# Softmax reciprocals of the first layer taken back from HBM as a tenth row instead of being spread by matmuls

## The chip, the cores and the metric

The kernel runs on one core of a Trainium2 chip. Its time is the device time of one execution in microseconds (us); a figure for a kernel is the median of several executions. The engines are called TensorE (PE in the profile, PEld where it loads weights), VectorE (DVE), ScalarE (ACT), GpSimd (POOL) and SyncE (SP, which issues the DMAs). All arithmetic is in 32-bit floats.

## The reference, cut to what matters

The network has four layers on two images of 512 channels by 64 x 64 pixels. The change touches only the first, an attention in which every pixel looks at its 3 x 3 neighbours (nine "taps") and at 256 pooled tokens. Both share one softmax, and to the weights of the nine taps a learned term is added:

```
attn_local = einsum('bhnd,bhndk->bhnk', q_scaled, k_local)          # 9 per pixel and head
attn_pool  = einsum('bhnd,bhpd->bhnp', q_scaled, l2norm(k_pool))    # 256 per pixel and head
attn = softmax(concatenate([attn_local, attn_pool], axis=-1), axis=-1)
a_local, a_pool = attn[..., :9], attn[..., 9:]
lt = einsum('bhnd,hdk->bhnk', q_norm, learnable_tokens) + learnable_bias + a_local
x_local = einsum('bhnk,bhndk->bhnd', lt, v_local)
x_pool  = einsum('bhnp,bhpd->bhnd', a_pool, v_pool)
out = (x_local + x_pool) @ W_proj + b_proj
```

There are 8 heads of 64 channels, so 128 channels (one partition each) hold two heads.

## The kernel before

The first layer of an image is cut into 16 units: four blocks of 128 channels by four stretches of 1024 pixels. It runs in **turns**. In one turn several generators, each working on another unit, are advanced in rotation, one `yield` at a time; one such rotation is a **step**, and a turn has ten of them, numbered 0 to 9 here. While `attend` works on unit u, `weigh` finishes unit u-1 and the projections prepare u+3 and u+4.

```
for i in range(-4, units + 1):
    k, q, ahead, u, before = (unit(i + n) for n in (4, 3, 1, 0, -1))
    stages = [norms, tap_products(ahead), attend(u), weigh(before), tap_sums(ahead), projections, normed, ...]
    in_turn(*stages)          # in rotation, one yield of each at a time
...
class Local: ...
    self.taps = [two parts of a lent buffer, one of its own]      # ring of three, 128 x 1024 each
    self.recip = part.take([P, TB])                               # TB = 512
def bank(self):               # a PSUM bank out of a pool of five
    return self.pp.tile([P, TB], F32, name="mm")
```

`attend` makes the exponentials of the pooled scores, their product with the values (`out`, not divided yet), and at step 7 the sum of all exponentials for each pixel and head, with the sums on 128 rows of `psD`: row 64j + r holds the pixels of half j, of head r mod 2. The exponentials of the taps, `el`, lie in 4 blocks of 32 rows; in each block the rows from 18 on belong to no tap. Their exponents are 0 and their learned term `lt` is 0, so after the two VectorE operations below such a row holds just the reciprocal.

```
    psD = sums()                                    # step 7 of attend
    for i in range(2):
        part = slice(i * TB // 2, (i + 1) * TB // 2)
        nc.vector.reciprocal(self.recip[:, part], psD[:, part])
    yield
    el = self.el.pop(u)                             # step 8
    nc.vector.tensor_tensor(el, el, self.recip, ALU.mult)
    nc.vector.tensor_tensor(el, el, self.lt.pop(u), ALU.add)
    self.spread = self.rows()                       # 64 x 1024 in HBM
    for j in range(2):
        nc.sync.dma_start(self.spread[:, j * TB:(j + 1) * TB], el[j * HD:(j + 1) * HD, :])
    self.fetch_tap(0)
    yield
    self.fetch_tap(1)                               # step 9
    yield

def fetch_tap(self, k):       # one HBM row to the 64 channels of each head
    at = 32 * (k % 2) + 2 * k
    for h in range(2):
        self.nc.sync.dma_start(self.taps[k % 3][h * HD:(h + 1) * HD, :],
                               bcast(self.spread[at + h], 0, HD))
```

`weigh`, a turn later, divides the pooled part by the sums, with the reciprocals spread over the channels by two matmuls of 2 rows, and adds the nine taps. A tap's weights are first copied by ScalarE into PSUM, then VectorE multiplies them with the shifted values `vx`, and GpSimd adds the product to `out`.

```
def weigh(self, u):
    out, R = self.out.pop(u), self.recip
    self.fetch_tap(2)
    yield                                           # end of step 0
    banks = [self.bank() for _ in range(2)]
    for j, ps in enumerate(banks):
        q = slice(64 * j, 64 * j + 2)
        nc.tensor.matmul(ps, self.cst[q, C_ROW:C_ROW + P], R[q, :], start=True, stop=True)   # L2260
    for j, ps in enumerate(banks):
        o = out[:, j * TB:(j + 1) * TB]
        nc.vector.tensor_tensor(o, o, ps, ALU.mult)                                          # L2263
    for k in range(9):                              # step 1 + k
        banks = [self.bank() for _ in range(2)]
        for ps, part in zip(banks, parts):
            nc.scalar.copy(ps, part)                                                         # L2270
        for j, (ps, part) in enumerate(zip(banks, parts)):
            nc.vector.tensor_tensor(part, vx[shifted by dy, dx], ps, ALU.mult)               # L2273
        nc.gpsimd.tensor_tensor(out, out, self.taps[k % 3], ALU.add)                         # L2277
        if k + 3 < 9:
            self.fetch_tap(k + 3)
        if k < 8:
            yield
    nc.sync.dma_start(self.yd[:, cc, lo:lo + self.UT], out)                                  # L2283
```

Other lines that the profile names: L133 the projections (128 x 128 weights, 512 columns), L1976 the output projection in the last turns, L2048 and L2055 the norms, L2138 and L2151 the tap products and their sums, L2183 and L2187 the pooled scores and their exponentials, L2193 the pooled values, L2230 the reciprocals, L2237 the store of the rows, L2247 the fetch of a tap. A 32-bit matmul stands as two instructions in the profile, so the two matmuls of L2260 are four records.

Of the kernel before, what the change touches and what calls it, by code (L numbers as in the profile page):

```python
# [11 lines left out]
ALU = mybir.AluOpType  # L12
# [3 lines left out]
P = 128  # L16
# [4 lines left out]
TB = 512  # L21
# [3 lines left out]
HD = 64  # L25
# [16 lines left out]
def bcast(ap, axis, n):  # L42

    a = ap.unsqueeze(axis)
    shape = list(a.shape)
    shape[axis] = n
    return a.to_broadcast(shape)
# [10 lines left out]
class General:  # L58
# [130 lines left out]
    def layer0(self, X, Y, sp_scale, tokT, d):  # L189
        tc, nc, vec = self.tc, self.nc, self.vec  # L190
        with tc.tile_pool(name="l0", bufs=1) as sp:
# [7 lines left out]
            with tc.tile_pool(name="l0b", bufs=2) as wp, \  # L199
                    tc.tile_pool(name="l0s", bufs=2, space=PSUM) as pps, \  # L200
                    tc.tile_pool(name="l0m", bufs=3, space=PSUM) as pp, \
                    tc.tile_pool(name="l0o", bufs=1, space=PSUM) as ppo:
                taps = wp.tile([18, 9, P], F32, name="taps", bufs=1)
                nc.sync.dma_start(taps, d["taps"])
                steps = []
                for cc in range(KC):
                    steps += self.local_chunk(X, Y, cc, xs, nmean, rstd, sp_scale, tokT, taps, d,
                                              wp, pps, pp, ppo)
                in_turn(steps[0][0]())
                for i, (_, attend) in enumerate(steps):  # L210
                    ahead = [steps[i + 1][0]()] if i + 1 < len(steps) else []
                    in_turn(attend(), *ahead)
# [63 lines left out]
    def local_chunk(self, X, Y, cc, xs, nmean, rstd, sp_scale, tokT, taps, d, wp, pps, pp, ppo):  # L276
# [137 lines left out]
        def attend(blk):  # L414
# [48 lines left out]
            nc.vector.tensor_tensor(Y[:, cc, blk * TB:(blk + 1) * TB], acc, psO, ALU.add)  # L463

        return [(lambda b=b: prepare(b), lambda b=b: attend(b)) for b in range(NB)]


# [1232 lines left out]
class Local:  # L1700
# [469 lines left out]
    def attend(self, u):  # L2170

        nc = self.nc
        cc = u // self.UN
        qs, el = self.qs[u % 3], self.el[u]
        out = self.att()
        prob = {}
        self.out[u] = out
        heads = [slice(h * HD, (h + 1) * HD) for h in range(2)]

        def exponentials(j, k2):  # L2180
            pS = [self.bank() for _ in range(2)]
            for h, c in enumerate(heads):
                nc.tensor.matmul(pS[h], self.kp[c, cc, k2 * P:(k2 + 1) * P],  # L2183
                                 qs[c, j * TB:(j + 1) * TB], start=True, stop=True)
            prob[j, k2] = [self.prob() for _ in range(2)]
            for h in range(2):
                nc.scalar.activation(prob[j, k2][h], pS[h], AF.Exp)  # L2187

        def values(j):
            psO = self.bank()  # L2190
            for k2 in range(2):
                for h, c in enumerate(heads):
                    nc.tensor.matmul(psO[c, :], self.vp[:, k2, cc * P + h * HD:][:, :HD],  # L2193
                                     prob[j, k2][h], start=(k2 == 0), stop=(k2 == 1))
            nc.scalar.copy(out[:, j * TB:(j + 1) * TB], psO)
            dst = prob[1, 1] if j else self.halves
            for h in range(2):
                nc.gpsimd.tensor_tensor(dst[h], prob[j, 0][h], prob[j, 1][h], ALU.add)  # L2198

        def sums():  # L2200
            psD = self.bank()
            blocks = [slice(j * HD, (j + 1) * HD) for j in range(2)]
            for h in range(2):
                for j, b in enumerate(blocks):
                    nc.tensor.matmul(psD[b, :], self.cst[:, C_EVEN + h:C_EVEN + h + HD],
                                     (prob[1, 1] if j else self.halves)[h], start=(h == 0),
                                     stop=False)
            for b in blocks:
                nc.tensor.matmul(psD[b, :], self.cst[b, C_SD:C_SD + HD], el[b, :], start=False,
                                 stop=True)  # L2210
            return psD

        exponentials(0, 0)
        yield
        exponentials(0, 1)
        yield
        values(0)
        yield
        exponentials(1, 0)
        yield  # L2220
        exponentials(1, 1)
        yield
        values(1)
        yield
        yield
        psD = sums()
# [5 lines that stand above are left out]
        el = self.el.pop(u)  # L2232
        nc.vector.tensor_tensor(el, el, self.recip, ALU.mult)
        nc.vector.tensor_tensor(el, el, self.lt.pop(u), ALU.add)
        self.spread = self.rows()
        for j in range(2):
            nc.sync.dma_start(self.spread[:, j * TB:(j + 1) * TB], el[j * HD:(j + 1) * HD, :])  # L2237
        self.fetch_tap(0)
        yield
        self.fetch_tap(1)  # L2240
        yield

    def fetch_tap(self, k):

        at = 32 * (k % 2) + 2 * k
        for h in range(2):
            self.nc.sync.dma_start(self.taps[k % 3][h * HD:(h + 1) * HD, :],  # L2247
                                   bcast(self.spread[at + h], 0, HD))

    def weigh(self, u):  # L2250

        nc = self.nc
        cc, y0 = u // self.UN, u % self.UN * self.UY
        out, R = self.out.pop(u), self.recip
        self.fetch_tap(2)
        yield
        banks = [self.bank() for _ in range(2)]
        for j, ps in enumerate(banks):
            q = slice(64 * j, 64 * j + 2)
            nc.tensor.matmul(ps, self.cst[q, C_ROW:C_ROW + P], R[q, :], start=True, stop=True)  # L2260
        for j, ps in enumerate(banks):
            o = out[:, j * TB:(j + 1) * TB]
            nc.vector.tensor_tensor(o, o, ps, ALU.mult)  # L2263
        for k in range(9):
            dy, dx = divmod(k, 3)
            parts = [self.taps[k % 3][:, j * TB:(j + 1) * TB] for j in range(2)]

            banks = [self.bank() for _ in range(2)]
            for ps, part in zip(banks, parts):
                nc.scalar.copy(ps, part)  # L2270
            for j, (ps, part) in enumerate(zip(banks, parts)):
                y = y0 + dy + j * self.UY // 2
                nc.vector.tensor_tensor(  # L2273
                    part.rearrange("p (y x) -> p y x", x=W),
                    self.vx[:, y:y + self.UY // 2, dx:dx + W],
                    ps.rearrange("p (y x) -> p y x", x=W), ALU.mult)
            nc.gpsimd.tensor_tensor(out, out, self.taps[k % 3], ALU.add)  # L2277
            if k + 3 < 9:
                self.fetch_tap(k + 3)
            if k < 8:  # L2280
                yield
        lo = u % self.UN * self.UT
        nc.sync.dma_start(self.yd[:, cc, lo:lo + self.UT], out)  # L2283
        yield
# [160 lines left out]
```

## Time and profile before

| what | value |
|---|---|
| time, median of 3 runs | 5462.01 us (5449.31 to 5468.27) |
| span of the profiled execution | 5449.6 us |
| mean granted TensorE clock | 0.969 of full speed |
| busy: TensorE, VectorE, ScalarE, GpSimd | 5161.0, 3144.7, 1793.0, 1803.2 us |
| first layer's turns with `weigh` in them, image 0 | from about 350 to 1075 us of the span |
| the same, image 1 | from about 3054 to 3776 us |
| distance from one turn's L2260 to the next, most turns | 45.86 us |

Busy times are unions of the records of an engine. The profile shows matmuls pipelined, with modelled ends, so two of them overlap in the records; where TensorE is concerned, the start of one group to the start of the next tells more than the length of a record. An instruction's "idle before" is the time that its engine stood still ahead of it, with the instruction that ended the wait.

### The profile page before, as it was taken

The page shows a single profiled execution, that of the slowest core. Times are in us where ns is not written, and L with a number is a line of the kernel's source. Part 1 is how long each engine was busy: PE and PEld are TensorE (multiplying, and loading weights), DVE is VectorE, ACT ScalarE, POOL GpSimd, SP SyncE. Part 2 cuts the span into 40 slices and gives each one's busy share as a digit, 9 for nine tenths or more (in the row PEclk, how much of TensorE's full clock was granted, in tenths as well). Part 3 has the DMA queues.
Part 4 walks back from the last instruction along what each step waited for, and adds up shares of the span by engine and source line. Part 5 has one row for each costly group of instructions (what it writes and reads, how often), then busy time and mean ns, then how long its engine had stood idle before and what let it go on. Part 6 is the DMA issues. An engine that isn't in the chain of part 4 may idle for free. (4 is left out here: it accounts for less than half of the span.)

```text
span 5449.6 us, 51666 instructions
## 1 busy us (share of the span) xinstructions
PE 5161.0 (95%) x18891; PEld 2254.2 (41%) x18891; DVE 3144.7 (58%) x3918; ACT 1793.0 (33%) x3409; POOL 1803.2 (33%) x1198
## 2 busy tenths in 40 slices
PE   7999999999988899999999999998999889999998
PEld 4423332554333344544444333335543334445443
DVE  3256667745679633565532566676456895334565
ACT  1245555233212233212212455542432131332221
POOL 0025556401310045444400355554012101554443
PEclk9999999999989999999989999999999899999999
DMA  3024445500000000211110344455000000000111
GB/s 141 2 62 122 128 126 154 153 18 24 1 1 0 1 1 1 82 35 57 51 55 2 81 126 125 124 154 154 1 24 0 1 0 1 1 8 20 38 36 42
DMA packets 113563, 293.27 MB, mean 54 GB/s; under 512 B 17234, under 2 KB 30034, under 8 KB 111252
## 3 DMA queue, kind: packets, MB, share of 16 engines
q1 hardware_dynamic: 113300, 289.88, 18.1%
q8 instruction: 151, 2.47, 0.2%
q14 instruction: 112, 0.92, 0.1%
HBM read 241.32 MB, written 48.50 MB: 53 GB/s over the span
## 5 line engine op out<-in xcount | busy, mean ns | idle before, releaser
L133 PE MATMUL mm<-big,w 128*128 128x512 f32 x2560 | 1188.4, 609 | 5.2 <-DVE late L2230 5.1
L133 PEld LDWEIGHTS mm<-big,w 128*128 128x128 f32 x2560 | 467.8, 191 | 687.4 <-issue 590.3
L2277 POOL TENSOR_TENSOR late<-late,big 128x1024 f32<-128x1024 f32 x192 | 454.7, 2368 | 298.6 <-DVE big L2273 285.3
L1265 POOL TENSOR_TENSOR total<-prob 128x512 f32<-128x512 f32 x128 | 159.6, 1269 | 759.3 <-ACT prob L1262 759.3
L1182 PE MATMUL acc<-big,dg 128*128 128x512 f32 x704 | 320.0, 613 | 59.0 <-DVE big L697 25.9
L1624 POOL TENSOR_SCALAR qf_sum<-qf,ksum_ratio 128x512 f32<-128x512 f32 x128 | 198.8, 1562 | 511.1 <-ACT qf L1674 353.8
L1437 POOL TENSOR_TENSOR big<-big 128x512 f32<-128x512 f32 x224 | 277.8, 1271 | 235.0 <-ACT big L1428 235.0
L2198 POOL TENSOR_TENSOR late<-late 128x512 f32<-128x512 f32 x128 | 160.6, 1276 | 487.1 <-ACT late L2187 448.2
L697 DVE TENSOR_TENSOR big<-big 128x3968 f32<-128x3968 f32 x72 | 308.8, 4289 | 6.9 <-ACT big L698 0.9
L2273 DVE TENSOR_TENSOR big<-big,mm 128x512 f32<-128x512 f32 x384 | 254.7, 679 | 85.1 <-ACT mm L2270 84.3
L1428 ACT ACTIVATE big<-mm,ed 128x256 f32<-128x256 f32 x512 | 193.7, 488 | 276.5 <-DVE top L1424 248.8
L2270 ACT COPY mm<-big 128x512 f32<-128x512 f32 x384 | 220.6, 594 | 161.4 <-DMA big<-rows 123.7
L1362 PE MATMUL mm<-proj,k 64*128 64x256 f32 x2048 | 268.9, 393 | 0.9 <-ACT k L1329 0.9
L1282 DVE RECIPROCAL recip<-psD 128x512 f32<-128x512 f32 x64 | 214.9, 3357 | 87.2 <-PE psD L1279 87.2
L1655 PE MATMUL mm<-k,w 128*128 128x512 f32 x512 | 242.0, 612 | 14.1 <-DVE k L1648 14.1
L1583 DVE TENSOR_REDUCE tops<-mm 128x2 f32<-128x512 f32 x256 | 161.5, 684 | 160.2 <-PE mm L1362 159.9
L1262 ACT ACTIVATE prob<-mm 128x512 f32<-128x512 f32 x256 | 132.0, 605 | 364.4 <-PE mm L1259 359.2
L1362 PEld LDWEIGHTS mm<-proj,k 64*128 64x128 f32 x2048 | 206.5, 188 | 105.7 <-issue 90.1
L2138 DVE TENSOR_TENSOR prod<-qs,big 128x1024 f32<-128x1024 f32 x192 | 230.5, 1215 | 30.7 <-PE tap L2151 29.1
L2277 POOL TENSOR_TENSOR late<-late,tap 128x1024 f32<-128x1024 f32 x96 | 226.5, 2360 | 64.4 <-DVE tap L2273 45.7
L133 PE MATMUL mm<-big,big 128*128 128x512 f32 x512 | 238.9, 629 | 0.0
L2151 PE MATMUL tap<-prod,cst 128*32 128x512 f32 x768 | 226.7, 612 | 9.9 <-DVE prod L2138 9.8
(364 smaller groups left out, 8300.2 us busy)
## 6 DMA issues: line engine op xcount, KB each, us to landing
big<-rows SPq DMA_DIRECT2D x384, 256.0 KB
tap<-rows SPq DMA_DIRECT2D x192, 256.0 KB
yd<-late SPq DMA_DIRECT2D x32, 512.0 KB
lost_all<-lost SPq DMA_DIRECT2D x128, 128.0 KB
out<-big SPq DMA_DIRECT2D x64, 256.0 KB
big<-in_W_kv SPq DMA_DIRECT2D x8, 1024.0 KB
rows<-late SPq DMA_DIRECT2D x64, 128.0 KB
big<-yd SPq DMA_DIRECT2D x16, 512.0 KB
```

Of the source, the lines that this page charges most:

```text
L133: self.nc.tensor.matmul(ps, w[:, kc, :], X[:, kc, blk * TB:(blk + 1) * TB], start=(kc == 0), stop=(kc == KC - 1))
L697: nc.vector.tensor_tensor(o, a, b, ALU.max)
L1182: nc.tensor.matmul(accs[b], dg, src[:, b * TB:(b + 1) * TB], start=(j == 0), stop=(j == 6))
L1282: nc.vector.reciprocal(r, psD)
L1362: nc.tensor.matmul(pS[h][i][:, t, :], k[lo:lo + HD, tok:tok + P], proj[lo:lo + HD, :], start=True, stop=True)
L1437: nc.gpsimd.tensor_tensor(a, a, part, ALU.add)
L1655: nc.tensor.matmul(ps, self.wo[:, kc, oc * P:(oc + 1) * P], qs[:, kc, :], start=(kc == 0), stop=(kc == KC - 1))
L2138: self.nc.vector.tensor_tensor(self.prods[k % 3].rearrange("p (y x) -> p y x", x=W), qs, self.kx[:, y + dy:y + dy + self.UY, dx:dx + W], A ...
L2151: nc.tensor.matmul(ps[32 * q:32 * q + 32, :], self.cst[:, C_TAPW + 16 - 2 * k:C_TAPW + 48 - 2 * k], self.prods[k % 3][:, j * TB:(j + 1) * ...
L2270: nc.scalar.copy(ps, part)
L2273: nc.vector.tensor_tensor(part.rearrange("p (y x) -> p y x", x=W), self.vx[:, y:y + self.UY // 2, dx:dx + W], ps.rearrange("p (y x) -> p y ...
L2277: nc.gpsimd.tensor_tensor(out, out, self.taps[k % 3], ALU.add)
```

## The change

The reciprocals are no longer spread by matmuls. As rows 20 and 21 of the stored rows hold them already, they are fetched back from HBM onto the 128 channels like a tap, and a turn of `weigh` handles ten rows in ten steps instead of nine in nine: the reciprocals in step 0, tap k in step k + 1 as before. The ring of three buffers stays, and turns on by one place from unit to unit, since ten is no multiple of three. The aim is to take the two matmuls off TensorE and to start `weigh` in the turn's first step.

```
-        self.fetch_tap(0)
-        yield
-        self.fetch_tap(1)
-        yield
+        self.fetch_tap(u, 0)
+        yield
+        self.fetch_tap(u, 1)
+        yield

-    def fetch_tap(self, k):
-        at = 32 * (k % 2) + 2 * k
+    def fetch_tap(self, u, i):
+        at = 32 * ((i - 1) % 2) + 2 * (i - 1) if i else 20
+        t = self.taps[(10 * u + i) % 3]
         for h in range(2):
-            self.nc.sync.dma_start(self.taps[k % 3][h * HD:(h + 1) * HD, :],
-                                   bcast(self.spread[at + h], 0, HD))
+            self.nc.sync.dma_start(t[h * HD:(h + 1) * HD, :], bcast(self.spread[at + h], 0, HD))

     def weigh(self, u):
-        out, R = self.out.pop(u), self.recip
-        self.fetch_tap(2)
-        yield
-        banks = [self.bank() for _ in range(2)]
-        for j, ps in enumerate(banks):
-            q = slice(64 * j, 64 * j + 2)
-            nc.tensor.matmul(ps, self.cst[q, C_ROW:C_ROW + P], R[q, :], start=True, stop=True)
-        for j, ps in enumerate(banks):
-            o = out[:, j * TB:(j + 1) * TB]
-            nc.vector.tensor_tensor(o, o, ps, ALU.mult)
-        for k in range(9):
-            dy, dx = divmod(k, 3)
-            parts = [self.taps[k % 3][:, j * TB:(j + 1) * TB] for j in range(2)]
+        out = self.out.pop(u)
+        self.fetch_tap(u, 2)
+        for i in range(10):
+            t = self.taps[(10 * u + i) % 3]
+            parts = [t[:, j * TB:(j + 1) * TB] for j in range(2)]
             banks = [self.bank() for _ in range(2)]
             for ps, part in zip(banks, parts):
                 nc.scalar.copy(ps, part)
+            dy, dx = divmod(i - 1, 3)
             for j, (ps, part) in enumerate(zip(banks, parts)):
+                if i == 0:
+                    o = out[:, j * TB:(j + 1) * TB]
+                    nc.vector.tensor_tensor(o, o, ps, ALU.mult)
+                    continue
                 ... (the tap's multiplication, as before)
-            nc.gpsimd.tensor_tensor(out, out, self.taps[k % 3], ALU.add)
-            if k + 3 < 9:
-                self.fetch_tap(k + 3)
-            if k < 8:
+            if i:
+                nc.gpsimd.tensor_tensor(out, out, t, ALU.add)
+            if i + 3 < 10:
+                self.fetch_tap(u, i + 3)
+            if i < 9:
                 yield
```

## The prediction

> **What bounds the kernel now.** I read the page first, then the busy times by stretch, then the kernel's lines that the change touches, and last the order of time over one turn. The page gives 95% to TensorE over the whole span, which hides the stages, so the stretch of nine even turns of image 0 comes next. Columns: stretch, its length, busy us and records of PE, PEld, DVE, ACT, POOL, clock, DMA share, GB/s.
>
> ```profile
> 440.00:854.00 414.00, 412.93 (x1482) 133.15 (x1480) 284.43 (x450) 232.96 (x406) 235.95 (x118) 1.00 0.48 128
> 992.00:1084.00 92.00, 85.63 (x209) 51.77 (x209) 67.15 (x107) 25.56 (x46) 48.71 (x23) 0.96 0.61 175
> ```
>
> In the even turns TensorE has work for 412.93 of 414 us, and the view of waits lists not one wait of a matmul there; the next engine, VectorE, has 284 us. So a turn lasts as long as its matmuls. In the last turns (second line) TensorE has gaps and the DMA share is up. Now the matmuls that are to go, and who waits for them:
>
> ```profile
> L2260 PE MATMUL mm<-late,cst x128: 587/640/693, 353.0 to 3737.6; 2*128 2x512 f32 x128
> ...
> who waited for it (us, times):
>   DVE late L2263: 242.6, 26
> ```
>
> 242.6 us of waiting looks like the prize. The order of time says otherwise. TensorE at the seam of two turns (the turn's step 0 begins near 624 us):
>
> ```profile
> 629.83 1.13 PE L2183 MATMUL mm<-big,kp 64*128 64x512 f32 x4
> 630.89 1.13 PE L2260 MATMUL mm<-late,cst 2*128 2x512 f32 x4
> 632.13 0.66 PE L2055 MATMUL mm<-cst,n_rows 128*128 128x128 f32 x4
> 632.80 1.94 PE L2193 MATMUL mm<-late,vp 128*64 128x512 f32 x8
> ```
>
> TensorE goes from group to group without a gap. L2260 holds its place from 630.89 to 632.13, that is 1.24 us, of which I count 0.18 to the passage into the small L2055, since L2183 ahead of it takes 1.06 from start to start. VectorE waits 10.21 us here because it has run ahead of TensorE and has nothing else to do; nobody is kept by it. What matters of L2260 is its place on TensorE: 1.06 to 1.24 us in a turn.
>
> ScalarE and the DMA queue at the same seam:
>
> ```profile
> 624.84 0.68 ACT L2016 ACTIVATE sq<-mm,b_q 128x512 f32<-128x512 f32 x1
> 625.41 1.08 ACT L2187 ACTIVATE late<-mm 128x512 f32<-128x512 f32 x2
> 628.94 0.69 ACT L2122 ACTIVATE big<-mm,b_v 128x512 f32<-128x512 f32 x1 [2.45 <-PE mm L133]
> ```
>
> ```profile
> 615.02 1.10 SPq L2237 DMA_DIRECT2D rows<-late  x2
> 617.97 2.63 SPq L2247 DMA_DIRECT2D big<-rows  x4
> 621.95 0.33 SPq L2283 DMA_DIRECT2D yd<-late  x1
> 622.38 1.30 SPq L2247 DMA_DIRECT2D tap<-rows  x2
> ```
>
> The rows are stored from 615.02, and the first fetch goes out at 617.97. After the exponentials of step 0 ScalarE stands still from 626.49 to 628.94.
>
> **What the Trainium skill says.** (1) "TensorE: Matmul & The Clock Gate", section "What a matmul computes" and its step-by-step part on the fill: the time of a matmul goes by the columns streamed, and the number of rows does not matter. The trace agrees: L2260 with 2 rows and L2183 with 64 rows both show 1.13 us for four records. So a matmul that only copies a row to 128 channels pays in full, and taking it away brings its full place. (2) "PSUM — Partial Sum Buffer", the four PSUM rules: DMA cannot reach PSUM. So the fetched reciprocals need a copy by ScalarE if VectorE is to read them there; L2270 shows 594 ns for one. (3) "DMA: Bandwidth & Descriptors", section on the anatomy of one DMA: a fixed part of about 2 us, most of it until the write is confirmed, and a reader has to wait for that. The trace agrees: 2.95 us from the issue of the first row store (615.02) to the first fetch (617.97), with two stores ahead of it. (4) "Perfetto Trace Analysis", section "Identifying the Most-Contended Engine": matmul busy time is a bad measure of headroom. Here I do not use it as one; that no matmul waits in nine turns is what tells.
>
> **The change, part by part.** There are 16 turns with `weigh` in each image, 32 in all.
>
> TensorE loses L2260. Turns whose length is set by TensorE: the nine even ones between 440 and 854 us and some four around them per image, by the distances from one L2260 to the next (45.86 us in nearly all of them, then about 40 where the projections run out, then 54 and 41). I take 13 per image, 26 in all. 26 x 1.06 = 27.6 us at least, 26 x 1.24 = 32.2 us at most; I take 1.15, so **-30 us**.
>
> VectorE keeps its two multiplications (684 ns each), with a copied row in PSUM as the second operand as before. They move from step 1 to step 0. It had stood idle for 10.21 us there, so the move is free, and it takes 1.4 us out of the crowd of step 1 to 3, where L2263 and L2273 follow one another without a gap from 632.05 on.
>
> ScalarE gets two copies more in a turn, 2 x 594 = 1.19 us. If they come after the exponentials of step 0 they fall into its 2.45 us of idle time: from 626.5 to 627.7, ahead of L2122. **0 us.** For this the row must be there by 626.5.
>
> The DMA gets one row more in a turn, two transfers of 256 KB. The row's fetch takes the place that tap 0 had, 617.97. How long a fetch takes I read from two whose landing ScalarE waited for: issued at 596.72, copy begun at 601.56; issued at 652.59, copy begun at 657.43; both 4.84 us. So the reciprocals land near 622.8, 3.7 us ahead of need. Tap 0 goes out at 619.5 and is needed at 632; tap 1 goes out at 622.4 and is needed at 633.4. Tap 2 is the tightest: its buffer is that of the reciprocals, so it goes out after their copies, at 627.7, lands near 632.5 and is needed at 635.45, or a microsecond or two earlier as the turn shrinks. It just fits. 128 GB/s over 45.86 us are 5.9 MB in a turn; two transfers of 256 KB more are 9%, at a DMA share of 0.48.
>
> What takes part of the gain back: in step 3 L2183 needs a bank, and its weight load is put down to VectorE's L2063 at 635.34. With TensorE 1.2 us earlier and VectorE only some 0.7 us earlier (its first tap product still hangs on ScalarE's copies behind the exponentials at 630.99), TensorE may wait 0.2 to 0.4 us in a turn, 26 x 0.2 = 5 us up to 10 us. I take **+6 us**.
>
> The last turns of an image: the view of waits for 990 to 1084 us puts ScalarE behind the fetches.
>
> ```profile
> ACT mm L2270 <- DMA big<-rows: 26.8, 9, 9.4
> ...
> ACT mm L2270 <- DMA tap<-rows: 6.3, 4, 2.1
> ```
>
> There the ring of three buffers sets the pace: fetch 4.8 us, copy, product, sum. A tenth row in that ring and 9% more bytes cost a microsecond or so in each of the last two or three turns; against it stands that in the last turn L2260 lies behind output matmuls and one L1976 then waits 4.14 us for L2263. That wait goes. I set the last turns at -1 to +3 us an image, together **+2 us**. The other layers are untouched.
>
> Sum: -30 + 6 + 2 = -22, from 5462 to **5440 us**.
>
> **The rivals.** *A new wait for the DMA.* The reciprocals now pass through store and fetch before step 0, while they were in place at once. If the copies are placed earlier on ScalarE than I think, say between L2166 (620.80) and L2014 (624.25), ScalarE stands up to 2 us until 622.8 and holds back the evacuation of the projections and so their banks. For it: the order on an engine is not that of the text (the small operations of `norms`, L2062 to L2070, alternate in the trace with tap products), so I can't know the place. Against it: 2.9 us of ScalarE's time ahead of L2014 is idle anyway. If all of 2 us came through in 26 turns: +52 - 30, so 5484 us. *The 242.6 us of VectorE were worth something.* Then step 1 to 3 would be quicker and TensorE's later waits would shrink; in the even turns there is none to shrink, so this could only be in the first two and last turns: at most 4 us each for eight turns, 5462 - 30 - 30 = 5400 us. *Banks.* Five banks serve all. Two are now taken in step 0 between the scores and a projection, and held until VectorE is through at about 628.4; two less are taken in step 1. If the scores of step 1 (629.83) hit a bank still held, it costs a microsecond a turn, and the time is the old one, 5462 us.
>
> **Range and chances.** The upside is bounded by TensorE's place of L2260, 32 x 1.24 = 40 us, plus the few waits of first and last turns; hence the low end of 5415. The high end, 5466, is the bank or half of the DMA rival. A change of 2% is 109 us, which neither the best nor the worst of these reaches: faster 0.02, same 0.94, slower 0.04.
>
> **What would show each step right or wrong.** L2260 absent, L2263's work in step 0, the distance between even turns down to about 44.9 us from 45.86 (right), or at 45.8 or more (a wait came in its place). In the view of waits: no matmul waiting in the even turns but 0.2 to 0.4 us at L2183. ScalarE's copies of the reciprocals without a wait for the DMA; a wait there of over 1 us in most turns would make the first rival true. In the last turns: ScalarE's wait for fetches near 33 us in 990 to 1084, or clearly more. I'd be wrong in kind if instructions unconnected with the change stood in another order, and their new order set the time.

## The result and the profile after

The kernel after takes **5435.18 us** (median of 4 runs, 5428.63 to 5439.51), the kernel before 5459.13 us in the same comparison (4 runs, 5449.31 to 5468.27). The ratio is 0.9955, with a 95% interval of [0.9934, 0.9977]. The predicted 5440 us is 5 us away, and 0.45% is far inside the 2% for which "same" stands. Much of what follows is about why that closeness is partly luck. The two profiled executions lie nearer together than the medians: spans of 5437.0 us after and 5449.6 us before. The figures by stage below are of single executions like these: in them after's first layer is 12 us shorter than before's over both images, where the medians differ by 24 us, with an interval from 13 to 36.

First the stretch of even turns that the prediction read, now of the kernel after (stretch, its length, busy us and records of PE, PEld, DVE, ACT, POOL, clock, DMA share, GB/s):

```profile
440.00:854.00 414.00, 412.05 (x1507) 137.37 (x1510) 302.06 (x477) 250.38 (x440) 244.91 (x122) 1.00 0.57 144
```

In the even turns TensorE is as full as before. More records fit into the same 414 us (1507 after 1482), though each turn has four fewer: the turns are shorter. The stretch of the last turns holds other work now, since all comes earlier, and is read below by its instructions. Next the multiplication by the reciprocals and what it waited for:

```profile
L2268 DVE TENSOR_TENSOR late<-late,mm x64: 676/684/690, 349.6 to 3725.7; 128x512 f32<-128x512 f32 x64
...
  ACT mm L2263: 55.2, 32
```

VectorE's 242.6 us of waiting for TensorE are gone, and 55.2 us of waiting for ScalarE's copies stand there. ScalarE and SyncE at the seam of two even turns of the kernel after:

```profile
703.37 1.08 ACT L2187 ACTIVATE late<-mm 128x512 f32<-128x512 f32 x2
707.31 1.11 ACT L2263 COPY mm<-tap 128x512 f32<-128x512 f32 x2 [2.86 <-DMA tap<-rows]
708.74 0.69 ACT L2122 ACTIVATE big<-mm,b_v 128x512 f32<-128x512 f32 x1 [0.33 <-PE mm L133]
```

```profile
695.95 1.11 SPq L2237 DMA_DIRECT2D rows<-late  x2
701.48 0.33 SPq L2282 DMA_DIRECT2D yd<-late  x1
702.29 1.11 SPq L2249 DMA_DIRECT2D tap<-rows  x2
```

The copies do stand between the exponentials and L2122, as predicted. But the fetch leaves 6.3 us after the row store (6.0 in most even turns) and not 2.95, for the store of the finished unit (L2282) stands ahead of it and waits for GpSimd's last addition. From 440 to 840 us SyncE's queue shows (total, times, longest):

```profile
SPq L2282 <- POOL late L2276: 38.5, 9, 4.8
```

So the row is late, and ScalarE waits 2.86 us in this turn, 2.5 to 3.3 us in the others.

**The even turns.** Each figure is the mean over eight even turns of image 0, from the start of one group on TensorE to the start of the next:

| us in one turn | before | after |
|---|---|---|
| distance of two turns | 45.86 | 44.02 |
| L2260, the spreading | 1.24 | 0 |
| L2151, tap sums | 6.75 in 6 groups | 5.78 in 5 groups |
| L2183, scores | 4.24 | 4.71 |
| L2193, values | 3.73 | 3.88 |
| L133, projections | 21.78 | 21.59 |

Image 1 has 45.88 and 44.33, so 44.17 us is the mean for after. The largest item beside L2260 is one that the change does not touch: **the tap sums take 0.97 us less**. The projections' 0.19 us are of the same kind, for y1 below, which changes the order alone, has 21.59 us too. The tap sums' 18 matmuls (36 records) are all still there. Two cuts from the views of TensorE show why, before and then after:

```profile
634.66 0.62 PE L2151 MATMUL tap<-big,cst 128*32 128x512 f32 x2
634.68 0.62 PE L2151 MATMUL tap<-prod,cst 128*32 128x512 f32 x2
635.12 0.60 PE L2151 MATMUL tap<-big,cst 128*32 128x512 f32 x2
635.13 0.60 PE L2151 MATMUL tap<-prod,cst 128*32 128x512 f32 x2
635.66 1.13 PE L2183 MATMUL mm<-big,kp 64*128 64x512 f32 x4
636.72 1.04 PE L2151 MATMUL tap<-prod,cst 128*32 128x512 f32 x2
637.69 3.70 PE L133 MATMUL mm<-big,w 128*128 128x512 f32 x8
```

```profile
747.72 0.62 PE L2151 MATMUL tap<-big,cst 128*32 128x512 f32 x2
747.73 0.62 PE L2151 MATMUL tap<-prod,cst 128*32 128x512 f32 x2
748.17 0.60 PE L2151 MATMUL tap<-big,cst 128*32 128x512 f32 x2
748.18 1.44 PE L2151 MATMUL tap<-prod,cst 128*32 128x512 f32 x6
749.56 3.70 PE L133 MATMUL mm<-big,w 128*128 128x512 f32 x8
```

A tap sum (form 128*32) writes one of four blocks of 32 rows: the two matmuls of tap k write blocks k mod 2 and 2 + k mod 2, so an even and an odd tap side by side fill all four. Four neighbours with four different blocks run at once: eight records from 634.66 to 635.66, 1.00 us. A lone one takes as long, 636.72 to 637.69, 0.97 us. That is in keeping with the Trainium skill, "TensorEngine Tiling (Array Packing)", section "Tiling Modes": tiles work independently and can run their matmuls in parallel. I call such a slot a **place**. In an even turn before, the tap sums stand in groups of 5, 1, 4, 1, 4 and 3 matmuls, the five in 1.81 us and each other group in 0.98 to 1.00: 7 places. After, they stand in groups of 1, 6, 3, 4 and 4, the six in 1.84 us and each other in 0.95 to 1.00: 6 places. No line of the tap sums was edited; the order in which instructions stand on an engine is settled when the program is built, and the edit to `weigh` shifted it over the whole layer.

**The last turns.** In the last turn of image 0 (kernel after; SyncE, ScalarE, TensorE):

```profile
1016.57 1.10 SPq L2237 DMA_DIRECT2D rows<-late  x2
...
1019.71 2.39 SPq L2249 DMA_DIRECT2D big<-rows  x4
```

```profile
1027.41 1.11 ACT L2263 COPY mm<-big 128x512 f32<-128x512 f32 x2 [10.85 <-DMA big<-rows]
```

```profile
1029.37 3.81 PE L1976 MATMUL mm<-sq,big 128*128 128x512 f32 x4 [9.61 <-DVE late L2268]
```

Store, fetch, landing and copy come one after the other, 10.84 us from the store to the copy, with nothing to fill them: TensorE waits 9.61 us for L2268. Before, it waited 4.14 us at that place. The turn ahead of it has 5.0 us more (L2193 for L2268). In image 1 these waits are 8.0 and 6.5 us, against 4.2 and none before.

### The profile page after: what moved, and what is told of

It is laid out like the page before. It is cut to its first block, busy times and chain, and to the rows that moved or that the text cites. A ratio compares the mean times of both kernels' runs of the same rounds, so it can differ in the third digit from the quotient of the medians.

```text
span 5437.0 us, 51556 instructions
## 1 busy us (share of the span) xinstructions
PE 5121.3 (94%) x18763; PEld 2252.8 (41%) x18763; DVE 3159.4 (58%) x3918; ACT 1824.3 (34%) x3473; POOL 1802.3 (33%) x1198
## 5 line engine op out<-in xcount | busy, mean ns | idle before, releaser
L133 PE MATMUL mm<-big,w 128*128 128x512 f32 x2560 | 1187.8, 611 | 9.4 <-DVE late L2230 9.4
L133 PEld LDWEIGHTS mm<-big,w 128*128 128x128 f32 x2560 | 472.2, 193 | 686.9 <-issue 585.6
L2263 ACT COPY mm<-big 128x512 f32<-128x512 f32 x428 | 244.6, 594 | 198.2 <-DMA big<-rows 164.7
L133 PE MATMUL mm<-big,big 128*128 128x512 f32 x512 | 239.0, 630 | 0.0
L1424 DVE TENSOR_REDUCE top<-mm 128x1 f32<-128x512 f32 x256 | 159.3, 684 | 131.4 <-PE mm L1362 131.1
```

Of the source, the lines that this page charges most:

```text
L133: self.nc.tensor.matmul(ps, w[:, kc, :], X[:, kc, blk * TB:(blk + 1) * TB], start=(kc == 0), stop=(kc == KC - 1))
```

## The experiments

The numbers by stage first, each from one profiled execution, images 0 / 1. "Turns 1 to 12" runs from the first unit's reciprocals (L2230) to the thirteenth's, "end" from there to the end of the layer. "Even turn" is the mean of eight. The second turn of x2 takes 43.04 us in image 0 and 47.83 in image 1, with the same order of instructions, so a sum over turns 1 to 12 is good to some 5 us.

| kernel | places | even turn | turns 1 to 12 | end |
|---|---|---|---|---|
| before | 7 | 45.86 / 45.88 | 545.8 / 546.5 | 222.2 / 219.7 |
| after | 6 | 44.02 / 44.33 | 533.7 / 531.0 | 228.1 / 229.7 |
| x1 | 6 | 43.99 / 44.69 | 528.7 / 536.7 | 223.5 / 220.3 |
| x2 | 6 | 44.04 / 44.33 | 527.8 / 534.5 | 227.1 / 229.8 |
| x3, no division | 8 | 45.51 / 45.51 | 540.8 / 548.0 | 216.1 / 219.8 |
| x4, matmuls more | 6 | 46.50 / 47.05 | 552.2 / 561.2 | 230.5 / 228.7 |
| y1, before reordered | 6 | 44.83 / 44.83 | 539.0 / 538.5 | 225.1 / 219.9 |
| y2, no division | 7 | 44.49 / 44.50 | 531.8 / 534.0 | 214.5 / 213.8 |
| y3, matmuls in step 0 | 8 | 46.57 / 46.72 | 555.1 / 558.4 | 222.4 / 222.1 |
| y4, after reordered | 7 | 44.96 / 44.92 | 541.2 / 541.3 | 229.7 / 228.4 |
| z1, store behind | 7 | 44.40 / 44.51 | 530.9 / 531.1 | 224.1 / 226.0 |
| z2, both | 7 | 44.42 / 44.60 | 530.8 / 527.6 | 220.2 / 217.4 |

My first theory was that the matmuls' place is the gain and the last turns take part of it back. The places came to light with x3.

### x1: the last two units keep the matmuls

```
+    def row_first(self, u): return 1 if u >= KC * self.UN - 2 else 0
     def weigh(self, u):
+        first = self.row_first(u)
+        if first:            # the two matmuls and L2263 of the kernel before, in step 1
-        for i in range(10):
+        for i in range(first, 10):
```

> The changed kernel, but the last two units of an image (14 and 15) get their reciprocals by the two matmuls again, in step 1 and with nine rows. Twelve turns from the first to the thirteenth reciprocals took 545.8 and 546.5 us (image 0 and 1) before and 533.7 and 531.0 after; from the thirteenth to the end of the layer 222.2 and 219.7 before, 228.1 and 229.7 after. Theory (the last turns lose because the reciprocals reach the channels only after store and fetch, which wait there behind other transfers): twelve turns as after, 534 and 531; the end as before, about 222 and 220; time some 16 us under the changed kernel, about 5419. Rival (the end is longer because the instructions stand in another order from the first turn on, whatever way the reciprocals take): the end stays at 228 and 230, time about 5435.

Measured: 5422.93 us, ratio 0.9937 [0.9922, 0.9953]. The end goes back to 223.5 and 220.3 us, and L1976's wait in the last turn to 4.2 us. The theory's number for the last turns held: the row costs them 4.6 and 9.4 us, 14 in all.

### x2: a buffer outside the ring for the last unit's row

```
+    def buffer(self, u, i):
+        if self.own(u) and i == 0:       # only unit 15
+            return self.qs[u % 3]
+        return self.taps[(10 * u + i - self.own(u)) % 3]
```

> The changed kernel, but for the last unit of an image the fetched reciprocals have a buffer of their own (one that is free by then), so its nine taps go through the ring of three from the start, as before the change. From the last reciprocals to the store of the last unit it took 47.1 and 47.5 us before and 52.9 and 49.6 after. Theory (late landing of the reciprocals): TensorE's wait for their multiplication in the last turn stays near 9.6 us in image 0, the stretch stays at 51 to 53 and 48.5 to 50, time within 3 us of 5435. Rival (a tenth row in the ring of three): the stretch falls to about 48 and 47.5, time about 5428.

Measured: 5429.86 us, ratio 0.9949 [0.9933, 0.9966]; after and x2 cannot be told apart by the time, nor the theory's 5435 us and the rival's 5428. With the row outside the ring, L1976's wait in the last turn stays (and L2193's one turn earlier is 7.0 us):

```profile
PE mm L1976 <- DVE late L2282: 9.8, 1, 9.8
```

From the last reciprocals to the store of the last unit it takes 50.7 and 50.0 us, near the theory's 51 to 53 and 48.5 to 50 and over 2 us above the rival's 48 and 47.5. So in the last turn it isn't the ring's three buffers that cost, it is the way through HBM; in x1, where that way is gone for these turns, the wait is back at 4.2 us.

### x3: the division left out

This kernel leaves out the division of the pooled part: no matmuls, no row, no multiplication, and a `weigh` of nine taps.

```
-        banks = ...; matmul(ps, ..., R[q, :]) x2 ; tensor_tensor(o, o, ps, ALU.mult) x2
         for k in range(9):
```

> The kernel before without the division of the pooled part: neither the two matmuls nor the two multiplications, and no fetch for them; this leaves out part of the computation. It shows what is to be had at most. Theory (the gain is TensorE's place of the two matmuls, and fetch, copies and multiplications of the change are hidden in the even turns): twelve turns as after the change, 531 to 535 us each image; the end at or below that of before, 215 to 222; time about 5420. Rival (fetch and copies cost something in the even turns too): twelve turns clearly shorter than after, 525 or less.

Measured: 5433.87 us, ratio 0.9953 [0.9936, 0.9969]. Even turns of 45.51 us fit **neither** theory: with all of the division away, they are 0.35 us shorter than before and 1.34 us longer than after. Broken down, L2260's 1.24 us are gone, but the tap sums take 7.72 us, in 8 places. So their order is what the next runs change.

### x4: the matmuls put back, with no reader

The kernel after, with the two matmuls of 2 rows issued in step 1 into banks that nothing reads.

```
+            if i == 1:
+                for j in range(2):
+                    q = slice(64 * j, 64 * j + 2)
+                    nc.tensor.matmul(self.bank(), self.cst[q, C_ROW:C_ROW + P], self.recip[q, :], start=True, stop=True)
```

> The changed kernel, with the two matmuls of two rows put back into step 1, into banks that nobody reads. Theory (TensorE's place is the gain): twelve turns back to about 545 us in each image, 24 x 1.06 to 1.24 = 25 to 30 us more over both, time about 5462. Rival (the gain is the earlier multiplication, which takes VectorE out of the crowd of step 1 to 3, or another order of instructions): twelve turns stay near 534 and 531, time near 5438.

Measured: 5493.72 us, ratio 1.0068 [1.0049, 1.0087]. The matmuls have their 1.24 us:

```profile
628.91 1.13 PE L2263 MATMUL mm<-late,cst 2*128 2x512 f32 x4
630.15 0.66 PE L2055 MATMUL mm<-cst,n_rows 128*128 128x128 f32 x4
...
644.90 3.70 PE L133 MATMUL mm<-big,w 128*128 128x512 f32 x8 [0.87 <-DVE tap L2276]
```

But a turn is 2.5 to 2.7 us longer than in after, twice that place. So the time is above both numbers that were foreseen. The last line shows a part of the rest: a projection waits for VectorE's tap product, which in before's and after's even turns it never does. By the distances from start to start, L2090, which stands ahead of that projection and whose slot takes in the wait, is 0.93 us longer than in after, in the mean; 0.37 us come back at the scores. The projections themselves are as long as in after in six of sixteen even turns (45.4 to 45.7 us each) and 1.6 to 1.7 us longer in the other ten (47.3 to 48.0 us).

x4 is not just after with two matmuls more. In its even turns the first fetch leaves 3.0 us after the row store and not 6.0, and a tap product stands between the two halves of the multiplication by the reciprocals. So the 1.24 us of the matmuls are shown; whether the rest comes from the two banks more or from the other order is not.

### y1 and y4: before and after with the tap sums in another order

In both, the calls of the tap sums are moved to other steps, and no other line is edited (y1 on before; y4 on after, with the two taps of a pair swapped as well).

```
-        sums(0), sums(1); yield; yield; sums(2), sums(3); yield; yield; ... sums(6), sums(7); yield; sums(8)
+        sums(0); yield; sums(1), sums(2); yield; yield; sums(3), sums(4); yield; yield; ... sums(7), sums(8)
```

> The kernel before the change, with the tap sums (L2151) given out in other steps: tap 0 in step 2, taps 1 and 2 in step 3, 3 and 4 in step 5, 5 and 6 in step 7, 7 and 8 in step 9. Nothing else differs; matmuls and their number are the same. The 18 matmuls of a turn write four blocks of 32 rows, and such that stand next to each other and write different blocks ran at once in the traces. Counted in the order of instructions, the even turns need 7 places of about 0.97 us for them before the change, 6 after it, 8 with the division left out, and the traces show 6.75, 5.78 and 7.72 us; this kernel needs 6. Theory (the order of the tap sums is worth about a place in the change's gain): even turns 45.86 - 0.97 = 44.9 us, 24 turns, time about 5436, the same as the changed kernel without any of the change. Rival (the places are no matter, the gain is the change's own): even turns 45.8, time about 5458.

> The changed kernel, with the tap sums given out in steps 2, 3, 5, 7 and 9, the later tap of a pair first. Nothing else differs. The order of instructions then has 7 places for the tap sums in an even turn, as many as the kernel before, in place of 6. Theory (the order is worth about a place in the change's gain): even turns 44.17 + 0.97 = 45.1 us, time 5435 + 23 = about 5458, no gain over the kernel before. Rival (the gain is the change's own): even turns 44.2, time about 5435.

Measured: y1 5440.09 us, ratio 0.997 [0.9961, 0.9979], with 44.83 us for an even turn. y4 5460.78 us, ratio 1.0013 [1.0005, 1.0021], with 44.94 us. So **before with 6 places is about as fast as after, and after with 7 places is no faster than before**. Each ratio is to the kernel before as measured beside that run: 5459.13 us beside after, 5456.23 beside y1 and y4. A 2 x 2 table of the ratios:

| | 7 places | 6 places |
|---|---|---|
| matmuls (before) | 1 | 0.9970 |
| row from HBM (after) | 1.0013 | 0.9955 |

Along a row the order is worth 0.3 to 0.6%; down a column the change itself is worth nothing that these intervals can separate at 6 places ([0.9934, 0.9977] against [0.9961, 0.9979]), and a trifle of loss at 7, 5460.78 against 5456.23 us.

Equal places are not quite equal orders. The projections take 21.59 us in y4 and 21.78 in before, the tap sums 5.78 us in after and 5.91 in y1, and in y4 the fetch leaves 6.9 us after the row store. The first two make the change look better than it is, by 0.19 and 0.13 us in an even turn.

### y2: the division left out, 7 places

As x3 (the division is left out), with the order of y1.

> The division left out, and with it part of the computation, as in the run before of that name, with the tap sums given out in steps 2, 3, 5, 7 and 9: 7 places of 0.97 us for them in an even turn in place of 8, as many as the kernel before has. So against the kernel before only the two matmuls and two multiplications are missing. Theory (the two matmuls have a place of 1.06 to 1.24 us): even turns 45.86 - 1.15 = 44.6 to 44.8 us against 45.51 with 8 places, time about 5411. Rival (TensorE's turn is set by something else and the matmuls leave hardly anything): even turns 45.5, time about 5434.

Measured: 5410.4 us, ratio 0.9913 [0.9886, 0.994], even turns 44.49 us. One place fewer than x3, 1.02 us fewer in a turn: 0.83 in the tap sums and 0.2 in the projections, which are shorter in this order. The theory of the places held. Beside before, with the same 7 places, it shows what the division costs, to within the 0.2 us by which the orders differ: 45.86 - 44.49 = 1.37 us in an even turn. The change took 0.92 of that (45.86 - 44.94, y4).

### y3: the matmuls and the multiplication in step 0

The kernel before, with the spreading in step 0 as in after, and no row fetched.

```
         self.fetch_tap(2)
-        yield
         banks = ...; matmul x2; tensor_tensor x2
+        yield
```

> The kernel before, with the two matmuls and the two multiplications of the division moved from step 1 to step 0; taps as before. It is the part of the change that begins in a turn's first step, without the fetch. The order of instructions has 8 places for the tap sums in an even turn, one more than before. Theory (places on TensorE set the even turns, an earlier start brings nothing there): even turns 45.86 + 0.97 = 46.8 us, time about 5480. Rival (the earlier start is what brings the gain, VectorE being free of the crowd in step 1 to 3): even turns at most 45.86, time 5455 or less.

Measured: 5474.18 us, ratio 1.0029 [1.0021, 1.0037], even turns 46.57 us, with 8 places. Against x3, which has 8 too, 46.57 - 45.51 = 1.06 us: the matmuls' bare place. Against before, the place more costs 0.97 us and L2260 and L2055 take 0.25 us less, which leaves nothing for the earlier start of the multiplication.

### z1 and z2: the store of the finished unit queued behind the fetch

z1 is the kernel after, z2 is x1, each with one constraint more on the order of SyncE's queue.

```
-        self.fetch_tap(u, 0)
+        self.fetched = self.fetch_tap(u, 0)
...
+        with issue_after(self.fetched):
             nc.sync.dma_start(self.yd[:, cc, lo:lo + self.UT], out)
```

> The kernel after; alone the store of the finished unit (L2282) is queued behind the fetch of the reciprocals on SyncE, where it stood ahead of it and waited for GpSimd's last addition. The tap sums stand as in the kernel after (6 places in nearly all even turns, 7 or 8 in one or two early ones: about 3 us more in all). Theory (the waiting store holds the fetch back by 3 us, ScalarE waits 2.8 us for its landing, and TensorE pays 0.6 to 0.8 us a turn through the banks): the fetch goes out about 3 us after the row store, ScalarE's wait for it falls under 0.5 us in the even turns, scores and values go back to 4.24 and 3.73 us, even turns 43.5 us from 44.17, total about 5423. Rival (the scores' and values' longer stretch comes from the banks that the copies hold, not from when the row lands): ScalarE's wait goes as well, even turns stay at 44.0 to 44.3, total about 5437.

> x1_matmul_in_last_two (the last two units of each image spread the reciprocals by matmuls) with the store of the finished unit queued behind the first fetch. Theory (store holds the fetch back): even turns 43.5 us, the last turns as in x1, total about 5409, under both kernels. Rival (banks, not the landing): even turns 44.2, total about 5425. In the last turns the store of a unit leaves a little later; if that matters, the stretch from the last store of a row to the end of the layer grows over the 49.6 and 47.4 us of x1.

Measured: z1 5428.84 us, ratio 0.9958 [0.9945, 0.9972], which is after's ratio; z2 5410.9 us, ratio 0.9927 [0.9914, 0.9941], the fastest of the kernels that compute everything. In z1 the fetch leaves 3.03 us after the store, and ScalarE goes from the exponentials to the copies without a gap (SyncE, then ScalarE):

```profile
732.09 1.10 SPq L2238 DMA_DIRECT2D rows<-late  x2
735.12 2.38 SPq L2250 DMA_DIRECT2D big<-rows  x4
737.62 0.51 SPq L2286 DMA_DIRECT2D yd<-late  x1
```

```profile
739.52 1.08 ACT L2188 ACTIVATE late<-mm 128x512 f32<-128x512 f32 x2
740.47 1.13 ACT L2266 COPY mm<-big 128x512 f32<-128x512 f32 x2
```

Scores and values fall from 4.71 and 3.88 to 4.43 and 3.74 us in image 0, by 0.42 us in a turn, and by 0.56 in image 1, where I expected 0.6 to 0.8. Yet the even turn is 44.40 us, not 43.5. The tap sums take 6.63 us: a seventh place has opened, and on TensorE this one opens by lateness (VectorE, then TensorE):

```profile
751.14 1.21 DVE L2139 TENSOR_TENSOR big<-qs,big 128x1024 f32<-128x1024 f32 x1
```

```profile
751.53 1.06 PE L2152 MATMUL tap<-prod,cst 128*32 128x512 f32 x6
752.41 1.05 PE L2152 MATMUL tap<-big,cst 128*32 128x512 f32 x2
```

VectorE's product is ready at 752.35. Three matmuls had gone at 751.53; the fourth, which would have run beside them, starts at 752.41 and takes a place of its own, 0.97 us. The lateness in turn goes with an order: on VectorE four tap products stand between the last tap's multiplication and that by the reciprocals in every even turn of after, in z1 three, and the fourth comes later. So z1 took the wait at ScalarE away, but changed VectorE's order with it, and the 0.42 and 0.56 us stand for both together. What it gained there, the seventh place swallowed.

z2 beats x1 by less than the two intervals can separate; its end is shorter, 220.2 and 217.4 us. The 49.6 and 47.4 us in its expectation are x1's times from the last reciprocals to the store of the last unit; z2 takes 48.2 and 47.1, so the later store cost nothing there.

## Why the prediction came out right, and which steps of it did not

**The number was right partly by chance.** With 7 places the same change gives 5461 against 5456 us, and with 6 places a ratio of 0.9955 against 0.9970. Of after's 0.45% the order alone brings 0.30% (y1), and what is left the intervals do not separate from nothing; my sum had nothing of the order. The prediction did say that it would be wrong in kind if instructions unconnected with the change stood in another order and set the time. That is what happened.

**TensorE, -30 us.** The mechanism is right, the place too: 1.24 us in before's even turns, 1.24 in x4, 1.06 in y3. At equal places an even turn gets 0.92 us (45.86 to 44.94) or 0.66 us (44.83 to 44.17) shorter. The sum is what is too large: over the turns 1 to 12 of both images, y1 to after is -5.3 - 7.6 = -12.9 us, before to y4 is -4.6 - 5.2 = -9.8 us, where -30 + 6 = -24 was predicted, for 26 turns. What before and after themselves show, -12.1 - 15.5 = -27.6 us, looks like the prediction and is mostly the order.

**Take-back, +6 us.** I put 0.2 to 0.4 us in a turn on the L2183 of step 3, as the bank's wait behind VectorE. Place and size are there in part. That L2183, which follows the first values, takes 1.27 us here in after from its start to the next group's, against 1.06 before:

```profile
758.69 1.35 PE L2183 MATMUL mm<-big,kp 64*128 64x512 f32 x4
759.96 0.63 PE L2151 MATMUL tap<-prod,cst 128*32 128x512 f32 x3
```

It does so in 12 of after's 16 even turns, and z1 keeps it (1.25 us), so this part is not the late row's; that a bank is behind it is not shown. The rest I had not foreseen: in the other four turns this L2183 takes 2.2 to 2.5 us, and in most of the 12 the second L2193 takes up to 0.7 us more. In z1 that rest is nearly gone. Together it is 0.62 us in a turn in image 0 and 0.81 in image 1 (L2183 and L2193), some 17 us in place of 6. In the view of waits almost nothing of it is to be seen, only in the distances from group to group.

**ScalarE's copies, "0 us".** This step failed. I took the fetch's departure, 2.95 us after the store, from a queue in which nothing stood between the two. In after the waiting L2282 stands there. The first rival named the right mechanism, a wait for the DMA ahead of L2122, and even its size at ScalarE (2 us foreseen, 2.5 to 3.3 measured). But of the 2.9 us TensorE felt about half a us (0.42 and 0.56, z1), because most of that time at ScalarE was idle before as well: the waits for L133 ahead of L2122 fell from 48.9 to 33.7 us between 440 and 840 us, and with the early row of z1 they are 62.7. So its 5484 us did not come.

**The last turns, +2 us.** Mis-sized. I took the tenth row for one more turn of the ring of three buffers; x2 gives it a buffer of its own in the last turn, and L1976's wait stays. What it costs is the way store, fetch, landing, copy, where before the sums were at hand: 222.2 and 219.7 us became 228.1 and 229.7, **+16 us**, and 13 to 16 us at equal places. And I expected L1976's 4.14 us of waiting to go; it became 9.61. With the turns' -12.9 or -9.8 us that makes the change worth nothing, or a few us of loss. The sign I had named for it, ScalarE's wait for fetches in 990 to 1084 us, does not show it: 31.7 us against 33.1, and 39.0 against 36.9 where the window is moved with the layer (960 to 1075 us after, 970 to 1085 before). What changed is that the copy behind the longest of them (10.85 us, 9.4 before) is now the one that L1976 hangs on.

**VectorE, 0 us.** Right: 187 us less of waiting brought no time that any run shows, and so the second rival (5400 us) fell. Banks, the third rival, gave its total at equal places (5462 predicted, 5461 in y4) but for another reason.

## What to carry to other kernels

Before you compare two versions, see whether unconnected instructions stand in the same order on the engine that sets the time; if not, make a pair that does, in both orders, or you measure the order. A value sent through HBM in place of two matmuls cost TensorE about half a us in a turn whose other work covers the way, and 13 to 16 us over the two images in the last turns, where nothing does; so treat the last turns apart, as x1 does. And look at what stands ahead of a fetch in its queue: a store that waits there holds it back.

## What the runs showed of the hardware that was not expected

- Matmuls that write different blocks of 32 rows and stand side by side share their time: four in 1.00 us, six in 1.84 us, one alone in 0.97 us. One whose data came 0.8 us after the others had started took 0.97 us of its own (z1).
- A store that waits for its data delays the transfers queued behind it: the fetch left 6.3 us after the row store with it ahead, 3.03 us with it behind.
- TensorE can lose time without a wait in the view: the third scores of an even turn take 1.28 us in place of 1.06 from start to start (after, against before), and for all of them between 440 and 840 us one wait of 0.2 us is listed.
